# Two mixture-of-experts stages: the second layer issued behind the next expert's first layer, turns two experts ahead

## The chip, the cores and the metric

The kernel runs on one core of one Trainium2 chip. A core has a matrix engine (TensorE, "PE" in the profile, its weight loads "PEld"), a vector engine ("DVE"), a scalar engine ("ACT"), a general engine ("POOL") and a sync engine ("SP") that here only issues transfers; each engine works through its own queue in order, and the engines wait for each other through semaphores. The metric is device time in microseconds (us) for one execution of the whole kernel; lower is better.

## The reference

Eight blocks follow each other on an activation x of 4 x 1024 x 128 (4096 tokens): gated linear attention, a mixture of experts, causal attention, the same mixture again, rotary attention, a dense feed-forward block, attention with linear biases, the same dense block. What matters here is the mixture:

```python
tokens = inputs.reshape(-1, H)                       # 4096 x 128
residual = tokens
tokens = _layer_norm(tokens, ln_gamma, ln_beta)
logits = tokens @ gate_weight.T
top1 = jnp.argmax(logits, axis=-1)                   # one of E = 8 experts
...
keep = rank < CAPACITY                               # CAPACITY = 256 rows per expert
dispatch = jnp.zeros((E, CAPACITY, H)).at[top1, slot].add(tokens * keep[:, None])
h = jax.nn.gelu(jnp.einsum('ech,ehi->eci', dispatch, wi), approximate=False)   # 128 -> 512
expert_out = jnp.einsum('eci,eih->ech', h, wo)                                 # 512 -> 128
combined = weight[:, None] * expert_out[top1, slot]
out = (residual + combined).reshape(inputs.shape)
```

So each expert takes 256 rows of 128 features through a layer to 512, a Gelu, and a layer back to 128. It happens twice in the kernel, each time in a stage of its own: the next block's normalisation needs every token.

## The kernel before

x stays in SBUF for the whole kernel as 32 tiles of 128 tokens. `dispatch` (L328) runs beside the attention that precedes a mixture: it normalises, gates and ranks the tokens and scatters the rows with indirect transfers into a DRAM tensor `slots`, 256 rows per expert. `experts` (L465) is the stage that changes. It is called twice, at L1362 (after the gated linear attention) and at L1372 (after the causal attention), each time with PSUM pools of its own: four single banks of 512 columns, handed out in turn by `k.bank()` (L60), and two pairs of banks handed out by `k.banks()` (L63).

For each of the 8 experts, in this order:

1. a load of the expert's 256 rows into `given` (L472, issued by SP, 128 KB, a buffer for each expert), which waits for all scatters;
2. two transposes on TensorE (L480) into a bank: the "turn";
3. the affine part of the normalisation on DVE, out of the bank into `givenT` (L482);
4. the first layer on TensorE (L485), 4 products of 256 columns into a pair of banks; in fp32 each product shows as two matmul passes in the profile, so "x8";
5. Gelu on ACT (L493), the pair of banks into `hid`;
6. the second layer (L497), 8 products of 128 columns into a bank, "x16" in the profile;
7. a copy on DVE out of the bank into `answer` (L505), and a transfer to the DRAM tensor `answers`, issued by ACT (L506).

`givenT`, `hid` and `answer` have two buffers each. After the experts, 32 indirect gathers on POOL (L510) fetch each token's row from `answers`, and DVE adds it, weighted, to x (L516). The framework orders each engine's instructions by the order in the program and by its own estimate of when their inputs are there, puts in the semaphore waits, and lets a tile in a reused buffer or pool wait for the last use of what lay there. In the first call ACT's queue also holds four loads of `halves` (L558) for the causal attention.

Of the kernel before, what the change touches and what calls it, by code (L numbers as in the profile page):

```python
# [13 lines left out]
F32 = mybir.dt.float32  # L14
# [6 lines left out]
P = 128  # L21
# [5 lines left out]
NE, CAP, NI = 8, 256, 512  # L27
# [437 lines left out]
def experts(k: Core, m: Experts, which, weights, pool):  # L465

    nc, x = k.nc, k.x
    answers = m.answers[which]
    for e, (wi, wo) in enumerate(weights):
        rows = slice(e * CAP, (e + 1) * CAP)  # L470
        given = pool.tile([P, CAP // P, P], F32, tag="given", name="given", bufs=NE)
        load = nc.sync.dma_start(given, m.slots[rows, :].rearrange("(a p) f -> p a f", p=P))  # L472
        for name in m.sent:
            k.tc.add_manual_dep(
                load.ins, name,
                mybir.DependencyInfo(mybir.DependencyClass.Sync, mybir.DependencyReason.DATA),
            )
        ps = k.bank()
        for a in range(CAP // P):
            nc.tensor.transpose(ps[:, a * P : (a + 1) * P], given[:, a, :], k.ident)  # L480
        givenT = pool.tile([P, CAP], F32, tag="givenT", name="givenT")
        nc.vector.tensor_scalar(givenT, ps[:, :CAP], m.gamma, m.beta, ALU.mult, ALU.add)  # L482
        hps = k.banks()
        for c in range(NI // P):
            nc.tensor.matmul(  # L485
                hps[:, c * CAP : (c + 1) * CAP],
                lhsT=wi[:, c * P : (c + 1) * P],
                rhs=givenT,
                start=True,
                stop=True,  # L490
            )
        hid = pool.tile([P, NI // P, CAP], F32, tag="hid", name="hid")
        nc.scalar.activation(hid.rearrange("p c s -> p (c s)"), hps, AF.Gelu)  # L493
        ops = k.bank()
        for a in range(CAP // P):
            for c in range(NI // P):
                nc.tensor.matmul(  # L497
                    ops[:, a * P : (a + 1) * P],
                    lhsT=hid[:, c, a * P : (a + 1) * P],
                    rhs=wo[:, c, :],  # L500
                    start=(c == 0),
                    stop=(c == NI // P - 1),
                )
        answer = pool.tile([P, CAP // P, P], F32, tag="answer", name="answer")
        nc.vector.tensor_copy(answer.rearrange("p a f -> p (a f)"), ops[:, :CAP])  # L505
        nc.scalar.dma_start(answers[rows, :].rearrange("(a p) f -> p a f", p=P), answer)  # L506

    for t in range(NT):
        got = pool.tile([P, P], F32, tag="got", name="got", bufs=4)
        nc.gpsimd.indirect_dma_start(  # L510
            out=got,
            out_offset=None,
            in_=answers,
            in_offset=bass.IndirectOffsetOnAxis(ap=m.slot[:, t : t + 1], axis=0),
        )
        nc.vector.scalar_tensor_tensor(  # L516
            x[:, t, :], got, m.weight[:, t : t + 1], x[:, t, :], ALU.mult, ALU.add
        )
# [816 lines left out]
def kernel(ctx: ExitStack, tc: tile.TileContext, a: dict, out: bass.AP):  # L1335
    k = Core(ctx, tc)
    dram = ctx.enter_context(tc.tile_pool(name="dram", bufs=1, space=bass.MemoryType.DRAM))
    with tc.tile_pool(name="moe_w", bufs=1) as wp:
# [20 lines left out]
        with tc.tile_pool(name="ca_pairs", bufs=1) as rows:  # L1359
            pairs = Pairs(k, rows, dram, "ca", 6, 1)  # L1360
            with k.psum("moe0", 4, 2), tc.tile_pool(name="moe0", bufs=2) as pool:
                experts(k, m[0], 0, weights[0], pool)  # L1362
            first.close()
            causal_attention(
                k, pairs, a["ca_wq"], a["ca_wk"], a["ca_wv"], a["ca_wo"],
                lambda pool, b: dispatch(k, m[0], pool, "1", b, ("d_z", "d_zT")),
            )
        with (
            k.psum("moe1", 4, 2), tc.tile_pool(name="moe1", bufs=2) as pool,
            tc.tile_pool(name="moe1_w", bufs=1) as weights,  # L1370
        ):
            experts(k, m[0], 1, m[0].load(k, weights), pool)  # L1372
# [147 lines left out]
```

## Time and profile before

| what | us |
|---|---|
| median of 3 runs (lowest to highest) | 2838.01 (2831.23 to 2841.02) |
| the profiled execution | 2828.45 |
| its span in the trace | 2826.7 |
| first experts stage: first turn to first gather | 331.53 to 389.29 |
| its gathers, to the last addition to x | 389.29 to 431.05 |
| second experts stage: first turn to first gather | 1447.64 to 1502.14 |
| its gathers, to the last addition to x | 1502.14 to 1544.89 |
| mean granted TensorE clock over the span | 0.887 |

The profile is one execution. Rows of its timeline give start, duration, engine, line and operation, and in brackets how long the engine had been idle and what released it. "PEclk" is the granted TensorE clock as a share of full speed. Time in the two experts stages counts in full towards the total where the first gather waits for the last answer.

### The profile page before, as it was taken

What the parts mean: (1) busy time and instruction counts of PE and PEld (TensorE: products, weight loads), DVE (VectorE), ACT (ScalarE), POOL (GpSimd) and SP (SyncE); (2) the same over time, 40 slices, a digit from 0 to 9 for tenths busy, and PEclk for the clock granted to TensorE, in tenths of its full rate; (3) what the DMA queues carried; (4) which work ended last, traced back from release to release, by engine and by line L of the source; (5) the groups of instructions that cost most, each with busy time, mean ns of one, the idle gap of its engine ahead of it and who ended that gap; (6) DMA issues with size and microseconds to landing.
All of it is one profiled execution on the core that took longest, in us unless ns stands there. A gap on an engine that the chain in (4) does not pass through costs nothing.

```text
span 2826.7 us, 40396 instructions
## 1 busy us (share of the span) xinstructions
PE 2262.1 (80%) x14251; PEld 1251.0 (44%) x14251; DVE 1651.9 (58%) x4807; ACT 1260.5 (45%) x2058; POOL 1080.2 (38%) x825
## 2 busy tenths in 40 slices
PE   4676336999989989989841799935999999998898
PEld 3554223444334334333331366723544454444666
DVE  4777117676766767764211665545776777772644
ACT  5542201354545544554320265620354555555775
POOL 3754330578667767768614233241000000000222
PEclk8888575899989989999976899975799999999999
DMA  4000113110110021000112100023210212000000
GB/s 126 29 9 8 38 36 121 45 52 17 56 59 17 17 83 32 17 23 2 60 32 60 54 1 1 1 56 107 83 47 16 91 32 91 28 6 2 5 12 16
DMA packets 71000, 112.25 MB, mean 40 GB/s; under 512 B 13868, under 2 KB 45870, under 8 KB 70786
## 3 DMA queue, kind: packets, MB, share of 16 engines
q1 hardware_dynamic: 57828, 93.18, 10.4%
q0 software_dynamic: 4096, 8.40, 1.0%
q10 hardware_dynamic: 8862, 7.95, 1.0%
q8 instruction: 118, 1.93, 0.3%
q14 instruction: 96, 0.79, 0.1%
HBM read 62.29 MB, written 42.99 MB: 37 GB/s over the span
## 4 chain that ended last, share of the span: by engine, by line
PE 50%; DVE 11%; issue 11%; POOL 8%; ACT 5%; DMA 4%; SPq 1%; ACTq 0%; POOLq 0%; DVEq 0%
PE bank L590 8%; PE o L994 7%; PE o L828 6%; PE bank L1247 6%; PE scores L590 6%; DVE nm L623 3%; POOL e_first L846 3%; DVE junk L618 3%; PE scores L596 2%; PE bank L792 2%; PE bank L777 1%; PE bank L497 1%; PE banks L485 1%; PE banks L1247 1%; PE bank L858 1%
## 5 line engine op out<-in xcount | busy, mean ns | idle before, releaser
L713 ACT ACTIVATE e<-scores 128x1024 f32<-128x1024 f32 (+3 forms) x704 | 544.7, 792 | 588.0 <-PE scores L596 352.8
L846 POOL TENSOR_TENSOR e_first<-e_first,e 128x1024 f32<-128x1024 f32 (+3 forms) x320 | 538.6, 1712 | 282.2 <-PE o L828 154.1
L618 DVE CUSTOM_DVE_ANT_0 junk<-bank,mask 128x128 f32<-128x128 f32 (+3 forms) x1024 | 495.4, 484 | 228.1 <-PE bank L590 161.4
L623 DVE TENSOR_REDUCE nm<-bank 128x1 f32<-128x512 f32 x512 | 331.3, 685 | 124.6 <-PE bank L590 119.3
L828 PE MATMUL o<-e,v 128*32 128x512 f32 (+3 forms) x2560 | 297.1, 493 | 0.0
L590 PE MATMUL bank<-aa_k,aa_q 62*128 62x512 f32 (+3 forms) x768 | 237.2, 429 | 44.1 <-DVE nm L623 26.4
L994 PE MATMUL o<-e,v 128*32 128x512 f32 (+3 forms) x1536 | 223.3, 508 | 0.0
L590 PE MATMUL bank<-ca_k,ca_q 62*128 62x512 f32 (+3 forms) x768 | 191.0, 419 | 28.4 <-DVE nm L618 13.9
L590 PE MATMUL scores<-ca_q,ca_k 64*128 64x512 f32 (+3 forms) x768 | 180.3, 445 | 40.1 <-ACT e L713 38.0
L590 PEld LDWEIGHTS scores<-ca_q,ca_k 64*128 64x128 f32 x768 | 77.0, 187 | 269.9 <-ACT e L713 189.6
L596 PE MATMUL scores<-halves 64*128 64x128 f32 x2048 | 195.5, 258 | 0.0
L596 PEld LDWEIGHTS scores<-halves 64*128 64x128 f32 x2048 | 189.0, 192 | 8.8 <-issue 0.5
L965 POOL TENSOR_TENSOR lo<-val,hi 128x512 fp32r<-128x512 f32 x16 | 20.1, 1273 | 423.5 <-ACT hi L964 401.5
L590 PEld LDWEIGHTS bank<-aa_k,aa_q 62*128 62x128 f32 x768 | 120.6, 200 | 108.9 <-DVE nm L623 54.7
L590 PE MATMUL scores<-aa_q,aa_k 64*128 64x512 f32 (+3 forms) x768 | 163.3, 409 | 2.7 <-ACT e L713 2.5
L1293 DVE TENSOR_TENSOR h<-val,h 128x512 fp32r<-128x512 f32 x128 | 90.6, 715 | 121.6 <-ACT h L1292 88.0
L1237 POOL CAST h<-gate 128x512 fp32r<-128x512 f32 x32 | 26.5, 828 | 340.9 <-DVE gate L1270 335.2
L866 DVE RECIPROCAL raw<-raw 128x128 f32<-128x128 f32 x128 | 117.5, 937 | 54.4 <-ACT raw L862 45.0
L1247 PE MATMUL bank<-h,ff_h1s 128*128 128x512 f32 x512 | 134.9, 411 | 12.4 <-POOL h L1241 8.8
L590 PEld LDWEIGHTS scores<-aa_q,aa_k 64*128 64x128 f32 x768 | 79.4, 190 | 133.0 <-issue 63.0
L1287 ACT ACTIVATE val<-bank,ff_t 128x512 f32<-128x512 f32 x128 | 87.9, 689 | 97.3 <-PE bank L1247 94.1
L590 PEld LDWEIGHTS bank<-ca_k,ca_q 62*128 62x128 f32 x768 | 96.6, 202 | 75.8 <-DVE nm L618 33.2
(277 smaller groups left out, 3916.7 us busy)
## 6 DMA issues: line engine op xcount, KB each, us to landing
ca_q<-ca_q SPq DMA_DIRECT2D x64, 128.0 KB
ca_k<-ca_k SPq DMA_DIRECT2D x64, 128.0 KB
aa_q<-aa_q SPq DMA_DIRECT2D x64, 128.0 KB
aa_k<-aa_k SPq DMA_DIRECT2D x64, 128.0 KB
wi<-in_moe_wi_dram SPq DMA_DIRECT2D x16, 256.0 KB
wo<-in_moe_wo_dram SPq DMA_DIRECT2D x16, 256.0 KB
ca_q<-hi SPq DMA_DIRECT2D x8, 512.0 KB
ca_q<-lo SPq DMA_DIRECT2D x8, 512.0 KB
```

What stands on the lines that cost most here:

```text
L590: self.k.nc.tensor.matmul(out, lhsT=lhsT, rhs=rhs, start=True, stop=stop, skip_group_check=True)
L596: self.k.nc.tensor.matmul(ps, lhsT=part[:, 0, :], rhs=part[:, 1, :], start=False, stop=(a == 1), skip_group_check=True,)
L618: nc.vector.tensor_tensor_reduce(junk[:, :cols], ps[:, :cols], self.mask[:, 512 - cols :], -1.0, 3e38, ALU.add, ALU.min, to,)
L623: nc.vector.tensor_reduce(to, ps[:, :cols], AX.X, ALU.max, negate=True)
L713: nc.scalar.activation(e[:, :, :w], ps[:, :, :w], AF.Exp, scale=scale)
L828: nc.tensor.matmul(outs[which][32 * i : 32 * i + 32, skip:], lhsT=v[:, j, i, 32 * which : 32 * which + 32], rhs=es[i // 2][:, i % 2, : 512 ...
L846: nc.gpsimd.tensor_add(to, to, es[i][:, :, : 512 - skip])
L866: nc.vector.reciprocal(part, part)
L994: nc.tensor.matmul(o[32 * i : 32 * i + 32, skip:], lhsT=v[:, j, 4 * r + i, :], rhs=es[i // 2][:, i % 2, : 512 - skip], start=(j == 0), sto ...
L1247: nc.tensor.matmul(ps, lhsT=weights[:, c, :], rhs=inputs[c][i], start=(s == 0), stop=(s == len(steps) - 1))
L1287: nc.scalar.activation(val, ps, AF.Gelu, scale=s[:, o : o + 1])
L1293: nc.vector.tensor_sub(nxt[1][:, o, :], val, hi.bitcast(F32))
```

## The change

It touches `experts` alone. All eight loads of `given` are issued first. The body of the loop is cut into three functions: `turned` (transposes and `givenT`, now three buffers), `inner` (first layer and Gelu) and `outer` (second layer, copy, transfer of the answer). A new loop calls them so that the turn of expert e+2 and the first layer of expert e+1 are issued ahead of the second layer of expert e. The transfer of an answer is issued by SP instead of ACT. What is computed, and the number of instructions of each kind, stay the same.

```diff
-    for e, (wi, wo) in enumerate(weights):
-        rows = slice(e * CAP, (e + 1) * CAP)
-        given = pool.tile([P, CAP // P, P], F32, tag="given", name="given", bufs=NE)
-        load = nc.sync.dma_start(given, m.slots[rows, :].rearrange("(a p) f -> p a f", p=P))
+    given = []
+    for e in range(NE):
+        t = pool.tile([P, CAP // P, P], F32, tag="given", name="given", bufs=NE)
+        load = nc.sync.dma_start(
+            t, m.slots[e * CAP : (e + 1) * CAP, :].rearrange("(a p) f -> p a f", p=P)
+        )
...
+        given.append(t)
+
+    def turned(e):
         ps = k.bank()
         for a in range(CAP // P):
-            nc.tensor.transpose(ps[:, a * P : (a + 1) * P], given[:, a, :], k.ident)
-        givenT = pool.tile([P, CAP], F32, tag="givenT", name="givenT")
+            nc.tensor.transpose(ps[:, a * P : (a + 1) * P], given[e][:, a, :], k.ident)
+        givenT = pool.tile([P, CAP], F32, tag="givenT", name="givenT", bufs=3)
         nc.vector.tensor_scalar(givenT, ps[:, :CAP], m.gamma, m.beta, ALU.mult, ALU.add)
+        return givenT
+
+    def inner(e, givenT):
         hps = k.banks()
...
         nc.scalar.activation(hid.rearrange("p c s -> p (c s)"), hps, AF.Gelu)
+        return hid
+
+    def outer(e, hid):
         ops = k.bank()
...
         nc.vector.tensor_copy(answer.rearrange("p a f -> p (a f)"), ops[:, :CAP])
-        nc.scalar.dma_start(answers[rows, :].rearrange("(a p) f -> p a f", p=P), answer)
+        nc.sync.dma_start(
+            answers[e * CAP : (e + 1) * CAP, :].rearrange("(a p) f -> p a f", p=P), answer
+        )
+
+
+    ready = [turned(0), turned(1)]
+    hid = inner(0, ready.pop(0))
+    for e in range(NE):
+        if e + 2 < NE:
+            ready.append(turned(e + 2))
+        nxt = inner(e + 1, ready.pop(0)) if e + 1 < NE else None
+        outer(e, hid)
+        hid = nxt
```

More of the change, by code (lines that the diff above doesn't have):

```diff
@@ L485, in experts @@
             nc.tensor.matmul(
[L486 to L490, printed above, removed]
+                hps[:, c * CAP : (c + 1) * CAP], lhsT=weights[e][0][:, c * P : (c + 1) * P], rhs=givenT,
+                start=True, stop=True,
             )
@@ L497, in experts @@
                 nc.tensor.matmul(
[L498 to L502, printed above, removed]
+                    ops[:, a * P : (a + 1) * P], lhsT=hid[:, c, a * P : (a + 1) * P],
+                    rhs=weights[e][1][:, c, :], start=(c == 0), stop=(c == NI // P - 1),
                 )
```

## The prediction

> **What bounds the kernel now.** I read the page first. No engine sets the whole span; the chain that ended last runs half over TensorE (PE), and each stage has its own limit. The two layers of the experts are in that chain with 1% each, so what can be won here is some tens of us at most:
>
> ```profile
> span 2826.7 us, 40396 instructions
> ...
> PE 50%; DVE 11%; issue 11%; POOL 8%; ACT 5%; DMA 4%; SPq 1%; ACTq 0%; POOLq 0%; DVEq 0%
> ```
>
> Then the chain in order of time inside the second experts stage. Columns: start, length, engine and operation. One expert is these pieces, one behind the other, and the next expert repeats them:
>
> ```profile
> 1472.24 2.07 PE bank L497 x16
> 1474.36 0.20 issue
> 1474.61 0.06 issue
> 1474.67 0.55 DVE givenT L482
> 1475.26 2.01 PE banks L485 x8
> 1477.35 1.03 ACT hid L493
> 1478.42 2.07 PE bank L497 x16
> ```
>
> From 1472.24 to 1478.42 is 6.18: second layer, turn, givenT, first layer, Gelu, with no two of them at once. The timeline of the first stage says the same with the idle times in brackets:
>
> ```profile
> 349.85 1.99 PE L485 MATMUL banks<-givenT,wi 128*128 128x256 f32 x8 [0.75 <-DVE givenT L482]
> ...
> 353.02 2.05 PE L497 MATMUL bank<-wo,hid 128*128 128x128 f32 x16 [1.17 <-ACT hid L493]
> ...
> 354.91 0.38 PE L480 MATMUL bank<-ident,given 128*128 128x128 f32 x2
> 355.11 0.42 DVE L505 COPY answer<-bank 128x256 f32<-128x256 f32 x1 [5.31 <-PE bank L497]
> 355.45 0.54 DVE L482 TENSOR_SCALAR givenT<-bank,gamma,beta 128x256 f32<-128x256 f32 x1
> ```
>
> PE idles twice per expert, 0.75 for givenT and 1.17 for Gelu; ACT and DVE idle over 5 in each 6.19. The stage is bound by the latency of one expert's chain. That its end counts is shown by the first gather, POOL idle until the last answer has landed:
>
> ```profile
> 386.05 0.42 DVE L505 COPY answer<-bank 128x256 f32<-128x256 f32 x1 [5.31 <-PE bank L497]
> 386.50 0.37 ACTq L506 DMA_DIRECT2D answers<-answer  x1
> 389.29 1.00 POOL L510 DMA_INDIRECT got<-answers,slot  x1 [49.44 <-DMA answers<-answer]
> ```
>
> After it come 32 gathers at 1.25, DVE's additions, and only then (431.73, 1545.09) the next block's loads on SP. Nothing runs beside that, so an earlier end moves all the rest forward.
>
> **The change, part by part.** *Order.* The built kernel has on PE: turns 0, 1, 2, first layers 0 and 1, second layer 0, then turn e+3, first layer e+2, second layer e+1, and so on, ending with first layer 7, second layers 6 and 7. On all other engines, and past the stage, the order is the old one. So Gelu(e) lies beside second layer e-1, turn e+2 and first layer e+1, and givenT(e+3) beside first layer e+2.
>
> What a dense expert costs PE, from pass to pass in the rows above: first layer (1.99-0.379)/7 = 0.230 a pass (0.379 is the median pass of L485), x8 = 1.84; second layer (2.05-0.275)/15 = 0.118, x16 = 1.89; turn 0.38-0.273 = 0.107, x2 = 0.21. Sum 3.95 against 6.19. Gelu has 1.89+0.21+1.84 = 3.94 of cover for its 1.02 and about 0.15 of hand-over; DVE's 0.42+0.54 lie under 3.95 too. Without that cover they return at 1.17 and 0.75 per expert. No buffer should bite: second layer e-1 has read its `hid` before Gelu(e+1) writes there; a pair of banks is read by Gelu(e) before first layer e+2; the third `givenT` buffer is what turn e+3 needs.
>
> *First stage.* Turn 0 is at 331.53 as before. Turn 2 now stands ahead of first layer 0 and needs the third load, issued 2 x 0.47 after the first; between 0 and 1.0 of delay, I take 0.2 (givenT has to be waited for anyway until 332.89). First layer 0 runs at half clock as before (3.63), first layer 1 right behind it until 338.4. Gelu 0 waits for the table load (1.28) and is over at 339.2, as before plus 0.2. From there PE is dense: 8 second layers, 6 first layers, 5 turns and the last pass's drain: 15.14+11.04+1.07+0.16 = 27.4, end 366.6 instead of 386.0 (383.96+2.05): 19.4 saved. That is more than 7 x 2.24 = 15.7 since the old stage also ran second layer 0 at half clock (3.25) and Gelu 1 behind `halves` (0.4 late). *Second stage.* The table is loaded early. First layer 0 from 1449.1, 3.70 at half clock, first layer 1 1.84, then 27.4: end 1482.0 instead of 1499.04: 17.0 saved.
>
> *Answers on SP.* Eight issues of 0.37 per stage leave ACT's queue, where only Gelus would have stood behind them (and those would have waited for an outer layer each, had they stayed). On SP they stand behind the eight loads (over at 331.4 and 1449.3, before any answer) and ahead of loads that today start 45 us after the last answer. SP's own rows for such an issue are 0.38 to 0.47: 0 to 0.1 per stage, I take 0.
>
> *Joints.* PE rows of this stage show semaphore instructions of 0.051; three per expert, if none is hidden, 1.2 per stage; none is seen between L497 and L480 in the row above (0.115 from pass to pass), so 0 taken, 1.2 kept as an end. *Pitch.* The dense stretch of the gated linear attention at 154.93 has 20 passes of 128 in 2.40, (2.40-0.275)/19 = 0.112; by that the two stages save 1.5 more.
>
> *Clock.* Both stages start at 0.50. Changes of the granted clock lie at 336.23, 339.64 and 343.06, worked out from half-us slices, 3.41 apart; PE idling from 336.5 to 339 cost one such slice of cold clock in the first stage. Dense work leaves no such hole; a start that misses a slice would cost half of 3.41 = 1.7 per stage. The Trainium skill (TensorE: Matmul & The Clock Gate, Part 1, The HAM clock gate) has a free-running window of about 3.4 us, and the 3.41 agrees. By the same page (Part 4, PE-mode transpose) turns do not count as busy, so turns 1 and 2 ahead of the first layer would not warm the clock: by it the 1.7 could fall due, by the row (first layer alone warmed it, 332.89 to 336.23) not.
>
> **Sum.** 19.4 + 17.0 = 36.4: the profiled execution's 2828.45 becomes 2792. It lies 9.6 under the median of the runs shown, 2838.0; against the median I expect 2802 (2838.0-36.4 = 2801.6).
>
> **Rivals.** *The clock stays cold under dense work (slower).* The trace has stretches where PE looks busy and is granted little, 41.73 of 47 us at 0.54:
>
> ```profile
> 368.40:374.60 6.20, 4.26 (x26) 3.47 (x26) 0.88 (x2) 1.02 (x1) 0.00 (x0) 1.00 0.07 21
> ...
> 460.00:507.00 47.00, 41.73 (x105) 20.69 (x103) 38.39 (x131) 4.09 (x6) 0.00 (x0) 0.54 0.19 50
> ```
>
> (Columns: window, length, busy PE, PEld, DVE, ACT, POOL, clock, DMA share, GB/s.) Cold, a first layer costs 3.68, a second 3.78, a turn 0.42: the 8, 6 and 5 of them are 54.4, the ends 395 and 1511, 9 and 12 later than today: 2838+21 = 2859. It turns from gain to loss when 36.4/57.5 = 63% of the stages is cold, a mean clock under 0.68. Against it the first row: 1.00 today with PE busy 69% and two holes per expert, all the way from 343. The page named has the mechanism that would do this in a section of its own (Part 1, A second HAM failure mode: psum-queue depth-cycling): small idles between groups that cycle through banks make the clock swing; no row of the experts after 343 shows that. 4%.
>
> *Only half of the overlap.* A buffer or a wait that I read wrongly keeps first layer e+1 behind Gelu(e): then only 0.75 of 14 periods goes, 10.5 in all: 2827.5. For it: several waits hang on buffers used in turn. Against it: the counts above. 6%.
>
> *Hidden anyway.* The gathers could wait for something else than the answers, as POOL's memsets in the first stage (to 339.9) or SP: 2838. The 49.44 of idle speaks against it. 3%.
>
> **How the numbers follow.** The forecast has 87%. Its own range: down by the pitch (1.5), up by 2 x (0.8 of start + 1.2 of joints + 1.7 of clock) = 7.4, so 2800 to 2809. The rest of the kernel is entered at another phase of the clock's slices; each change of clock that falls a slice earlier or later moves it by 1.7, and the long cold stretches at 460 and 1940 to 2008 (0.50) end in such a change. The runs shown differ by 9.8 with no change at all. I add 7 above and 10 below, since the profiled execution lies that much under the median: 2790 to 2816. About 0.3%, 8.5 us, is what a measurement of this kernel can tell from no change. Faster by more: the forecast and most of the half overlap (its 10.5 is just over), 0.92; within: 0.04; slower: the cold clock, 0.04.
>
> **What would show it.** Right: from the second answer on, an expert every 3.95 on PE with no idle over 0.1 ahead of L493 and L505 (new lines of the layers), clock 1.00, Gelu over at least 2 us before its second layer; the first stage from first turn to first gather near 38.4 instead of 57.8, the second near 37.5 instead of 54.5; 32 gathers at 1.25 unchanged. Wrong: a period near 5.4 with ACT releasing PE (half overlap), a period near 7.9 with clock 0.5, or stages shorter by 36 with the same total, which would mean that a later stage gave it back.

## The result, and the profile after

| | before | after |
|---|---|---|
| median (lowest to highest) of 4 runs each | 2835.44 (2831.23 to 2841.02) | 2788.81 (2786.61 to 2798.8) |
| the profiled execution, its span | 2828.45, 2826.7 | 2786.61, 2784.8 |
| first experts stage, first turn to first gather | 57.76 | 36.93 |
| second experts stage | 54.50 | 35.12 |
| span outside both stages | 2714.4 | 2712.8 |

The ratio is 0.9844, with a 95% interval of 0.9822 to 0.9866: faster by 1.3 to 1.8%. The median lies 1.2 below the low end of the predicted range, which was set against a median before of 2838.01; as a ratio that range is 0.983 to 0.992, and the measured ratio lies in it. Of the 41.9 by which the two spans differ, the stages hold 40.2 (20.8 and 19.4), and 1.7 lies elsewhere.

The stage windows of the changed kernel's profile (window, its length, then busy PE, PEld, DVE, ACT, POOL, granted clock, DMA share, GB/s): the first stage, its gathers, the second stage.

```profile
333.36:370.29 36.93, 33.18 (x208) 30.17 (x208) 7.10 (x16) 9.36 (x9) 8.54 (x15) 0.92 0.18 48
370.29:412.10 41.81, 0.00 (x0) 0.00 (x0) 11.24 (x32) 0.00 (x0) 30.24 (x32) 0.50 0.18 50
1430.75:1465.87 35.12, 32.04 (x208) 29.44 (x208) 7.11 (x16) 8.18 (x8) 0.01 (x1) 0.94 0.18 51
```

PE runs the same 208 passes as before, now busy for 33.18 of 36.93 us where it was busy for 37.60 of 57.76, by the same window of the kernel before:

```profile
331.53:389.29 57.76, 37.60 (x208) 30.17 (x208) 7.20 (x16) 9.47 (x9) 8.32 (x14) 0.93 0.11 29
```

The gathers still take 41.81 (41.76 before): nothing was given back there. What changed inside is seen in the chain of waits in order of time, in the second stage (start, length, engine and operation):

```profile
1440.78 1.78 PE bank L505 x16
1442.56 0.22 PE bank L485 x2
1442.78 1.73 PE banks L493 x8
1444.51 1.78 PE bank L505 x16
```

Between these rows the chain no longer goes through DVE or ACT. From 1440.78 to 1444.51 one expert takes 3.73 (6.18 before), and the three pieces, second layer, turn and first layer, fill it. The timeline of the first stage shows where the other two engines went (in brackets the idle time ahead and what ended it):

```profile
346.63 0.38 PE L485 MATMUL bank<-ident,given 128*128 128x128 f32 x2
346.83 0.42 DVE L510 COPY answer<-bank 128x256 f32<-128x256 f32 x1 [2.86 <-PE bank L505]
346.85 1.89 PE L493 MATMUL banks<-givenT,wi 128*128 128x256 f32 x8
347.17 0.53 DVE L487 TENSOR_SCALAR givenT<-bank,gamma,beta 128x256 f32<-128x256 f32 x1
348.58 1.95 PE L505 MATMUL bank<-wo,hid 128*128 128x128 f32 x16
348.84 1.02 ACT L498 ACTIVATE hid<-banks 128x1024 f32<-128x1024 f32 x1 [2.71 <-PE banks L493]
350.36 0.38 PE L485 MATMUL bank<-ident,given 128*128 128x128 f32 x2
```

The PE rows carry no bracket. `givenT` (347.17 to 347.70) lies beside a first layer that does not need it, and Gelu (348.84 to 349.86) beside the second layer of the expert before; the second layer that needs it begins at 352.31, some 2.4 later. That the end of the stage still counts in full is shown by POOL's wait for the last answer:

```profile
370.29 1.00 POOL L527 DMA_INDIRECT got<-answers,slot  x1 [28.39 <-DMA answers<-answer]
```

### The profile page after: what moved, and what is told of

The parts are those of the page before. It is cut to its first block, busy times and chain, and to the rows that moved or that the text cites. A ratio compares the mean times of both kernels' runs of the same rounds, so it can differ in the third digit from the quotient of the medians.

```text
span 2784.8 us, 40381 instructions
## 1 busy us (share of the span) xinstructions
PE 2246.4 (81%) x14251; PEld 1247.6 (45%) x14251; DVE 1649.4 (59%) x4807; ACT 1259.7 (45%) x2058; POOL 1080.5 (39%) x825
## 4 chain that ended last, share of the span: by engine, by line
PE 49%; issue 12%; DVE 12%; POOL 8%; ACT 4%; DMA 3%; SPq 1%; ACTq 0%; POOLq 0%; DVEq 0%
PE bank L607 8%; PE o L1011 7%; PE o L845 6%; PE scores L607 6%; PE bank L1264 6%; POOL e_first L863 3%; DVE nm L640 3%; DVE junk L635 3%; PE scores L613 2%; PE bank L809 2%; PE bank L794 1%; PE banks L493 1%; PE bank L505 1%; POOL h L1258 1%; PE bank L875 1%
## 5 line engine op out<-in xcount | busy, mean ns | idle before, releaser
L845 PE MATMUL o<-e,v 128*32 128x512 f32 (+3 forms) x2560 | 293.1, 487 | 0.0
L607 PE MATMUL bank<-aa_k,aa_q 62*128 62x512 f32 (+3 forms) x768 | 235.1, 425 | 41.9 <-DVE nm L640 26.8
L1011 PE MATMUL o<-e,v 128*32 128x512 f32 (+3 forms) x1536 | 220.9, 504 | 0.0
```

The source lines that it names most:

```text
L607: self.k.nc.tensor.matmul(out, lhsT=lhsT, rhs=rhs, start=True, stop=stop, skip_group_check=True)
L845: nc.tensor.matmul(outs[which][32 * i : 32 * i + 32, skip:], lhsT=v[:, j, i, 32 * which : 32 * which + 32], rhs=es[i // 2][:, i % 2, : 512 ...
L1011: nc.tensor.matmul(o[32 * i : 32 * i + 32, skip:], lhsT=v[:, j, 4 * r + i, :], rhs=es[i // 2][:, i % 2, : 512 - skip], start=(j == 0), sto ...
```

## The experiments

The theory: the time went because Gelu (1.17 of PE's idle time per expert) and `givenT` (0.75) left PE's path, each by its own half of the change. The rivals: that one half did it all, that the loads issued together or the answers on SP did it, and that the gain comes from the clock at the start. In every run the two stages are read from the trace, from first turn to first gather, since the rest of the kernel is of no fixed length (below).

### The two halves alone, in program order

Turns two ahead, each expert's second layer behind its own first:

```diff
-    hid = inner(0, ready.pop(0))
     for e in range(NE):
         if e + 2 < NE:
             ready.append(turned(e + 2))
-        nxt = inner(e + 1, ready.pop(0)) if e + 1 < NE else None
-        outer(e, hid)
-        hid = nxt
+        outer(e, inner(e, ready.pop(0)))
```

> The program text has the turns two experts ahead and the second layer directly behind its own first layer, and the framework may order TensorE's queue: it puts three of the four products of the next first layer ahead of the second layer. Theory A: what counts is the built order, not the text: cover of 3 x 0.43 = 1.30 for a Gelu hole of 1.17, period 3.7 to 3.8, stages within 1 of 36.9 and 35.1, time as with the whole change. A theory by which the written order itself is needed: as strict_turns, 5.2.

The second layer late, each turn just ahead of its own first layer:

```diff
-    ready = [turned(0), turned(1)]
-    hid = inner(0, ready.pop(0))
+    hid = inner(0, turned(0))
     for e in range(NE):
-        if e + 2 < NE:
-            ready.append(turned(e + 2))
-        nxt = inner(e + 1, ready.pop(0)) if e + 1 < NE else None
+        nxt = inner(e + 1, turned(e + 1)) if e + 1 < NE else None
         outer(e, hid)
         hid = nxt
```

> The text has the second layer behind the next first layer and turns just one expert ahead; the framework splits the second layer around the next first layer, with the turn ahead of its first half. Theory A: Gelu is covered by half a second layer and a turn, 0.90 + 0.22 = 1.12 against 1.17, givenT by half a second layer, 0.90 against about 0.75, or with the answer's copy ahead of it on DVE up to 1.2: period 3.7 to 4.2, stages 37 to 41 and 35 to 39, time 0 to 8 above the whole change. If the written depth of two is what counts: as strict_late, 4.8.

Measured: turns alone 2792.82 (ratio 0.9848, 0.9828 to 0.9868), stages 39.10 and 37.48; late second layers alone 2792.43 (0.9851, 0.9831 to 0.9871), stages 39.28 and 38.38. Each half alone gives most of it: 35.7 and 34.6 of the 40.2 that the stages of the whole change give. The turns alone missed what was expected (stages within 1 of the whole change) by more than 1 in both stages: the period is 3.88 and not 3.73, and a hole is left at the end. The late second layers alone, with a period of 4.06, lie inside what was expected. The reason is the order that the framework chose. On PE, with the turns two ahead in the program, it puts three of the four products of the next first layer ahead of a second layer by itself; only the last expert, which has no next one, shows Gelu's hole (PE rows of that kernel's timeline):

```profile
353.16 2.05 PE L505 MATMUL bank<-wo,hid 128*128 128x128 f32 x16
355.05 0.38 PE L485 MATMUL bank<-ident,given 128*128 128x128 f32 x2
...
362.59 0.60 PE L493 MATMUL banks<-givenT,wi 128*128 128x256 f32 x2
364.36 2.05 PE L505 MATMUL bank<-wo,hid 128*128 128x128 f32 x16 [1.17 <-ACT hid L498]
```

With the late second layer alone it puts half of a second layer between a turn and its first layer, which hides `givenT`:

```profile
352.94 0.38 PE L485 MATMUL bank<-ident,given 128*128 128x128 f32 x2
353.38 1.16 PE L505 MATMUL bank<-wo,hid 128*128 128x128 f32 x8
354.38 1.89 PE L493 MATMUL banks<-givenT,wi 128*128 128x256 f32 x8
```

So these two runs do not separate the halves. The order had to be forced.

### The two halves alone, in a forced order

The program orders as above, and each matrix product of the two layers (in the second kernel the turns too) is bound behind the one issued before it, by a dependency that orders and adds no semaphore:

```diff
+    def put(made, behind):
+        if behind and done:
+            k.tc.add_manual_dep(
+                made.ins, done[-1],
+                mybir.DependencyInfo(mybir.DependencyClass.NoSync, mybir.DependencyReason.DATA),
+            )
+        if behind:
+            done.append(made.ins.name)
```

> Turns two experts ahead, but TensorE is held to the second layer of expert e directly behind its own first layer. Theory A (two separate holes on TensorE, each closed by what is issued into it): the hole for givenT goes, the hole for Gelu (1.17) stays. Period 1.89 first layer with its drain + 1.18 wait + 1.89 second layer + 0.22 turn = 5.2 against 6.19 before and 3.73 with the whole change; stages from first turn to first gather near 49 and 46 (57.8 and 54.5 before, 36.9 and 35.1 with the whole change); time about 18 below the kernel before. Theory B (the gain comes from the loads issued first and from the answers' transfers leaving ACT's queue, which this kernel has too): period near 3.7, stages near 37 and 35. Theory C (it is the unbroken stream that counts, any hole left brings the old speed back): period near 6.2.

> The second layer behind the next first layer, but each turn only directly ahead of its own first layer, TensorE held to that order. Theory A: the hole for Gelu goes, the hole for givenT (0.75) stays: period turn to first layer 1.13 + first layer 1.84 + second layer 1.79 = 4.76; stages near 45 and 42.5; time about 24 below the kernel before. Theory B: period near 3.7, stages near 37 and 35. Theory C: near 6.2.

Turns two ahead, second layer right behind its own first layer (PE rows of its timeline), a period of 5.17:

```profile
356.08 2.05 PE L516 MATMUL bank<-wo,hid 128*128 128x128 f32 x16 [1.17 <-ACT hid L509]
357.97 0.38 PE L496 MATMUL bank<-ident,given 128*128 128x128 f32 x2
358.19 1.89 PE L504 MATMUL banks<-givenT,wi 128*128 128x256 f32 x8
361.25 2.05 PE L516 MATMUL bank<-wo,hid 128*128 128x128 f32 x16 [1.17 <-ACT hid L509]
```

Second layer late, turn right ahead of its own first layer, a period of 4.75 (351.95 to 356.70):

```profile
351.95 1.99 PE L504 MATMUL banks<-givenT,wi 128*128 128x256 f32 x8 [0.75 <-DVE givenT L498]
...
355.57 0.38 PE L496 MATMUL bank<-ident,given 128*128 128x128 f32 x2
356.70 1.99 PE L504 MATMUL banks<-givenT,wi 128*128 128x256 f32 x8 [0.75 <-DVE givenT L498]
358.53 1.95 PE L516 MATMUL bank<-wo,hid 128*128 128x128 f32 x16
```

Each kernel keeps exactly the hole that its half does not close. The two savings per expert, 6.19 - 5.17 = 1.02 and 6.19 - 4.75 = 1.44, add up to 2.46, which is the whole change's 6.19 - 3.73. Each saving is 0.27 more than the idle time in its bracket (0.75 and 1.17): a hole also costs the 0.16 by which the last pass ahead of it is longer than its pitch (a turn's row is 0.38 long, yet work that needs no wait starts 0.22 after it), and the first pass behind it takes 0.10 longer (1.99 against 1.89). In the stages: 50.34 and 47.02 for the first kernel, 43.46 and 43.28 for the second, against 57.76 and 54.50; savings of 14.9 and 25.5, together 40.4, against 40.2 for the whole change. In time: 2812.35 (ratio 0.9923, 0.9891 to 0.9954) and 2811.81 (0.9921, 0.9898 to 0.9943). The first gained more in time than in its stages, but its interval, 13 to 31 us, holds the 14.9.

### What came along with the change

The old order with the loads first, three `givenT` buffers and the answers on SP:

```diff
+    for e in range(NE):
+        outer(e, inner(e, turned(e)))
```

> The loads of what is given first, answers issued by SP, three givenT buffers, but the old order of turn, first layer, second layer. Theory A: no gain from these: period 6.19, stages 57.8 and 54.5, at most 0.4 less in the first, where Gelu 1 no longer stands behind an answer; time as before, within 2. Theory B: most of the gain, stages near 37 and 35.

The whole change with the answers left on ACT:

```diff
-        nc.sync.dma_start(
+        nc.scalar.dma_start(
             answers[e * CAP : (e + 1) * CAP, :].rearrange("(a p) f -> p a f", p=P), answer
         )
```

> The whole change, but the answers' transfers stay on ACT. As the prediction had it: each Gelu behind them would wait for a second layer, some 0.4 to 1.8 per expert that TensorE can't cover: stages up to 10 longer. Rival: the transfer of answer e is ready 0.45 after second layer e, Gelu e+2 is wanted only after turn and first layer (0.22 + 1.89), so nothing waits: period 3.73, stages 36.9 and 35.1, time as the changed kernel within 2.

And the changed kernel once more beside them:

> The changed kernel once more, as the measure for the others of this group: 44 to 47 below the kernel before, stages 36.9 and 35.1.

The first: 2834.89, ratio 0.9992 (0.9981 to 1.0003), and a period of 6.19 as before:

```profile
357.55 2.05 PE L505 MATMUL bank<-wo,hid 128*128 128x128 f32 x16 [1.17 <-ACT hid L498]
...
363.74 2.05 PE L505 MATMUL bank<-wo,hid 128*128 128x128 f32 x16 [1.17 <-ACT hid L498]
```

Its second stage took 54.58 (54.50 before). Its first took 60.08, where 57.8 or a little less was expected: the clock stood at 0.50 from 342.8 to 353.0 (from 339.6 to 343.1 in the kernel before), so that the second expert's layers took 3.78 and 3.56 instead of 1.99 and 2.05. So without the new order the rest is worth nothing. The second: 2799.4, 0.9865 (0.9846 to 0.9884), with stages of 36.94 and 35.85, beside 2796.64, 0.9847 (0.9827 to 0.9866), with stages of 36.93 and 36.01 for the changed kernel. The stages do not differ by more than those of the changed kernel do between profiles, so the move to SP shows no worth either, and ACT's rows in the kernel with the answers on ACT say why:

```profile
352.10 1.02 ACT L498 ACTIVATE hid<-banks 128x1024 f32<-128x1024 f32 x1 [2.71 <-PE banks L493]
354.28 0.37 ACTq L511 DMA_DIRECT2D answers<-answer  x1
355.83 1.02 ACT L498 ACTIVATE hid<-banks 128x1024 f32<-128x1024 f32 x1 [2.71 <-PE banks L493]
```

A Gelu behind an answer in the queue waits for a first layer that PE runs after that answer's second layer. The issue is over at 354.65, and the Gelu's input comes at 355.83 anyway.

### The start of a stage

From first turn to first second layer (that of expert 0) the changed kernel takes 7.65 in the first stage and, in three profiles, 6.13 to 7.02 in the second: cold passes, and in the first stage a table load on ACT. Two idle things were added to take both away: products of 512 columns whose result nobody reads, ahead of the turns, and a Gelu of one column that loads the table early.

```diff
+    ps = k.bank()
+    for _ in range(19 if which == 0 else 16):
+        nc.tensor.matmul(
+            ps, lhsT=k.ident, rhs=x[:, 0:4, :].rearrange("p t d -> p (t d)"), start=True, stop=True
+        )
+    early = pool.tile([P, 1], F32, tag="early", name="early", bufs=1)
+    nc.scalar.activation(early, m.gamma, AF.Gelu)
```

> The changed kernel with 19 and 16 idle products of 512 columns on TensorE while the scatters run (their result is not read) and a Gelu on one column that brings the table in early. If the rest of the loss is the cold start: first layer 0 at 0.22 a pass instead of 0.46 and no table load on the path: first second layer about 4.5 after the first turn instead of 7.6 and 6.1, stages near 33.8 and 33.5, time 4 to 5 below the changed kernel. If the clock is cold again by the first turn, or the idle products delay it: stages as before, time the same or up to 2 longer.

Measured: 2796.05, ratio 0.986 (0.9842 to 0.9879). The second layer came 4.67 and 4.86 after the first turn, as expected, and the second stage took 33.85. But the first stage took 39.44, longer than without. Its timeline:

```profile
338.21 1.95 PE L514 MATMUL bank<-wo,hid 128*128 128x128 f32 x16
...
344.72 1.94 ACT L507 ACTIVATE hid<-banks 128x1024 f32<-128x1024 f32 x2 [7.01 <-DMA halves<-low]
345.79 3.59 PE L514 MATMUL bank<-wo,hid 128*128 128x128 f32 x16 [3.69 <-ACT hid L507]
```

Gelu 1 stands on ACT behind the four `halves` loads, which are issued at 342.21, once POOL has made their input `low` (341.79 to 342.18), about when the changed kernel issues them too (341.93). There they stand behind Gelu 1 and cost next to nothing (below); here PE waits 3.69, falls back to half clock, and runs a second layer in 3.59. Four runs took this apart: the same with the `halves` loads issued by POOL, the changed kernel as the measure beside it, the changed kernel with only those loads moved, and idle transposes in the place of the idle products (with no early Gelu).

```diff
-                nc.scalar.dma_start(
+                (nc.gpsimd if name == "ca" else nc.scalar).dma_start(
```

```diff
+    for _ in range(88 if which == 0 else 76):
+        nc.tensor.transpose(ps[:, :P], x[:, 0, :], k.ident)
```

> The kernel with the idle products and the early one-column Gelu, and with the four halves transfers of the causal pair issued on POOL's queue instead of ACT's. If the halves transfers are what held Gelu 1 (7.01 us idle ahead of it, 3.69 of PE behind it), the first stage is as short as the second, about 33.8 us from first turn to first gather (39.44 with them on ACT), the second stays at 33.9, and the two together are 4 to 5 below the changed kernel's 36.9 and 35.1 to 36.0. The rival, that the early Gelu itself or the load of its table makes the hole: the first stage stays near 39.4. The time may hide either, since the time outside the stages has differed by 11 us between executions.

> The changed kernel once more, as the measure beside the others: stages of 36.9 and 35.1 to 36.0 us, a median between 2787 and 2799.

> The changed kernel with the four halves transfers on POOL's queue alone. Its own Gelu 1 stood 3.23 us behind them by the trace, but its second layer came up to 0.48 us late only at one place, so stages of 36.9 and 35.1 to 36.0 are expected by one theory; by the rival, that these transfers hold the Gelus of the changed kernel's first stage too, the first stage is shorter by 0.5 to 1.5 us.

> The changed kernel with idle transposes of 128 columns (88 ahead of the first stage, 76 ahead of the second) in the place of the idle products of the kernel with the early Gelu, and no early Gelu. If transposes warm the clock as products do, the granted clock is 1.00 when the first layer of expert 0 starts, its 8 passes take 1.9 and not 3.6 us, and the first second layer of the second stage starts about 4.9 us after the first turn (4.86 with products, 6.13 without). If transposes don't count as work (the Trainium skill, TensorE: Matmul & The Clock Gate, Part 4, says so of PE-mode transposes), the clock stays at 0.50 past that point, the 8 passes take 3.6 us, and the second layer starts about 6.1 us after it.

Measured, with each stage split at its first second layer:

| kernel | first stage | second stage | time |
|---|---|---|---|
| kernel before | 7.50 + 50.26 | 6.09 + 48.41 | 2835.44 |
| changed kernel, first profile | 7.65 + 29.28 | 6.13 + 28.99 | 2788.81 |
| changed kernel, second | 7.66 + 29.27 | 7.02 + 28.99 | 2796.64 |
| changed kernel, third | 7.43 + 29.27 | 6.74 + 28.98 | 2795.77 |
| idle products, early Gelu | 4.67 + 34.77 | 4.86 + 28.99 | 2796.05 |
| the same, `halves` on POOL | 4.67 + 29.00 | 5.11 + 29.37 | 2790.61 |
| `halves` on POOL alone | 6.96 + 29.11 | 6.76 + 29.33 | 2795.79 (one run) |
| idle transposes | 6.94 + 29.27 | 7.01 + 28.99 | 2784.98 (one run) |

The kernel before starts its stages as the changed one does, so the gain is not in the start: it lies behind the first second layer. There 1.6 of the first stage's 21.0 is what the old kernel lost in that stage alone, a second layer and a turn at half clock (1.3) and Gelu 1 behind the `halves` loads (0.3).

With `halves` on POOL the first stage is 33.67 instead of 39.44: the loads were the cause. The two stages together take 68.15, against 72.05 to 72.94 in the three profiles of the changed kernel, the least of any run. Its time, 2790.61 (ratio 0.9853, 0.9834 to 0.9873), cannot be told from 2795.77 (0.9851, 0.9826 to 0.9877), taken beside it. With only the `halves` loads moved the first stage is 0.6 shorter than in the third profile, a size that the rival had named; but 0.5 of it lies ahead of the first second layer, where no Gelu stands behind these loads, and 0.16 behind it. So the loads hold the changed kernel's own first stage by 0.2 at most. In both kernels with these loads on POOL the second stage is longer by 0.34 and 0.38 behind its first second layer (29.33 and 29.37 against 28.99); it comes between the last copy on DVE and the first gather (3.39 and 3.42 against 3.05), and why was not looked into.

The idle transposes missed their aim, since they were over 6.7 and 6.3 us before the turns, but the clock answered all the same. Windows of half a microsecond of that kernel (PE busy, granted clock, DMA share, GB/s):

```profile
311.50:312.00 0.50, 0.50 (x5) 0.50 0.00 0
...
316.50:317.00 0.50, 0.50 (x5) 0.60 0.36 123
317.00:317.50 0.50, 0.50 (x7) 1.00 0.00 0
...
323.50:324.00 0.50, 0.20 (x2) 1.00 0.00 0
...
326.50:327.00 0.50, 0.00 (x0) 1.00 0.00 0
327.00:327.50 0.50, 0.00 (x0) 0.64 0.07 16
```

PE did nothing but transposes from 311.04 (88 show as 88 passes, where each fp32 product shows as two), and the clock rose at 316.9, 5.9 later. With idle products in the place of the transposes, behind the same small products of the gating, it was 311.88 and 317.8, the same 5.9 (4.5 to 5.5 in the three other stretches of idle products). So the transposes warmed the clock as products do; then PE stood idle from 323.7, the clock fell at 327.1, and the first layer ran cold (3.06 and 3.78 in the two stages). The first layer was cold, as the second of the two outcomes laid down has it, but for another reason than the one given there.

### The rest of the kernel

Span less both stages, in every profile of this study:

| kernel | us |
|---|---|
| before | 2714.4 |
| changed kernel, three profiles | 2712.8, 2722.0, 2724.6 |
| the eight others with the framework's order | 2718.8, 2711.7, 2714.6, 2718.7, 2711.7, 2712.8, 2721.8, 2711.1 |
| the two in a forced order | 2712.3, 2722.8 |

One and the same kernel differs by 11.8. The stages differ by 0.9 in these three profiles, so it is not there. Two windows late in the kernel, in the attention with linear biases, of its first profile and then of its third:

```profile
2100.00:2200.00 100.00, 94.64 (x737) 50.62 (x733) 76.23 (x241) 52.98 (x77) 5.02 (x4) 1.00 0.21 73
2400.00:2500.00 100.00, 95.35 (x721) 48.82 (x719) 72.44 (x236) 53.05 (x75) 0.00 (x0) 1.00 0.04 13
```

```profile
2100.00:2200.00 100.00, 94.69 (x702) 49.72 (x694) 73.07 (x226) 49.34 (x72) 5.03 (x4) 0.95 0.21 71
2400.00:2500.00 100.00, 95.67 (x691) 48.53 (x683) 70.06 (x229) 50.51 (x72) 0.00 (x0) 0.95 0.05 15
```

At equal PE busy time fewer passes fit in where the mean clock of the 100 us was 0.95 instead of 1.00. From the first start to the last, the products of L1011 take 620.9 in the first profile, 627.2 in the second, 636.6 in the third, at mean clocks of 0.98, 0.96 and 0.95. Why the clock falls in one execution and not in another was not tried.

## Why the prediction was right, and where it was off

*The bound and the mechanism* held. The latency of one expert's chain set the stages, Gelu and `givenT` went under cover, and the forced orders show each half closing its own hole, 1.44 and 1.02 per expert.

*The period was mis-sized*: 3.95 was predicted, 3.73 measured (1.78 + 0.22 + 1.73). The step that failed is "What a dense expert costs PE, from pass to pass". It took its pitches from rows that follow a wait, and the first pass of such a burst is 0.10 longer than the others. The old kernel's timeline had one cut out:

```profile
356.04 0.48 PE L485 MATMUL banks<-givenT,wi 128*128 128x256 f32 x1 [0.75 <-DVE givenT L482]
```

That is 0.48 for a pass of 0.378. Behind other work the first layer shows 1.89 instead of 1.99, the second 1.95 instead of 2.05, so the dense pitches are (1.89 - 0.379)/7 = 0.216 and (1.95 - 0.275)/15 = 0.112, not 0.230 and 0.118. The 27.4 of dense work was 26.0 (341.01 to 367.03): 1.4 per stage, 2.8 in all. The prediction had the 0.112 from a dense stretch of another block, worth 1.5, but used it for the low end of its range only; that row was the better one.

*The start of the first stage* was right: 7.67 from first turn to first second layer worked out, 7.65 measured. *The start of the second* was worked out at 7.0 (first layers of 3.70 and 1.84 behind a turn), and measured at 6.13, 7.02 and 6.74: a spread of 0.9, less than the 1.7 set aside for the phase of the clock.

*The sum.* 36.4 predicted, 40.2 in the two stages of the first profile, 39.3 and 39.8 in the others. 2.8 of the 3.8 missing is the pitch, 0.9 the second start. The stages were named as 38.4 and 37.5 and came out at 36.93 and 35.12.

*Answers on SP* was taken at 0, and is 0. The sentence in brackets, that the Gelus behind them would have waited for a second layer each had they stayed, is wrong: the run with the answers on ACT lost nothing.

*Joints* at 0 held: the chain's pieces follow each other without one.

*The clock.* It did not stay cold under dense work: 1.00 from 339.0 on in the first stage, so that rival falls. It also stayed at 1.00 in the forced order with a hole of 1.17 per expert (PE busy 23.39 of 30 us):

```profile
345.00:375.00 30.00, 23.39 (x152) 1.00 0.09 25
```

The Trainium skill's mechanism for swings between short groups (TensorE: Matmul & The Clock Gate, Part 1, A second HAM failure mode: psum-queue depth-cycling) is thus not met at these holes. The Trainium skill's sentence that transposes do not count as busy in the same way (TensorE: Matmul & The Clock Gate, Part 4, PE-mode transpose) does not agree with the idle fp32 transposes here, under which the clock went from 0.50 to 1.00 after 5.9 us in one stage and 5.7 in the other.

*Half of the overlap* and *hidden anyway* fell with the period of 3.73 and the gather that still waits for the last answer. The period of a kernel with only `givenT` hidden, which the rival put near 5.4, is 5.17 in the forced order: the rival took off the bracket of 0.75 alone, where the hole costs 1.02.

*The total.* The range's width came from the rest of the kernel, and rightly: 11.8 between profiles of one kernel. The medians of the changed kernel in three sets of runs were 2788.81, 2796.64 and 2795.77; the first is 1.2 under the range, and the other two inside it. They lie 46.6, 40.2 and 38.4 under the medians of the kernel before in the same sets (the second had been expected 44 to 47 under). The stages hold 40.2, 39.3 and 39.8 of that, so some 6 of the first set's 46.6 were luck: more than the stages gave, and within the scatter of the rest.

## What to carry to other kernels

Where a stage is a chain of two products with a step of another engine between them, put the neighbour's product into the hole, and count the gain as the holes times the number of items. The savings of the two holes added up to that of both (1.02 + 1.44 = 2.46), but the trace's idle brackets alone (0.75 + 1.17 = 1.92) fall short of it: take a hole from start to start of the work on either side, against the same work running dense. Take the cost of a dense stretch from rows that follow other work on the engine, since a row behind a wait holds its first pass's extra. Before moving anything earlier, look at what else is in the queues it crosses: the `halves` loads cost 0.2 at most until the first second layer came 3 us sooner and Gelu 1 stood behind them, and then 5.8.

## What the runs showed of the hardware

- The first matrix pass behind a wait of PE takes 0.10 longer than the next, for 256 columns (0.48 against 0.378) and, from the rows of 2.05 and 1.95, for 128.
- Fp32 transposes raised the clock as products did: it rose 5.9 and 5.7 us after the first of a run of transposes, 4.5 to 5.9 us after the first of a run of products (four stretches). It fell 3.4 and 4.6 us after the last transpose.
- The same kernel's long attention stretch took 620.9 to 636.6 from execution to execution, at mean clocks of 0.98 to 0.95: a scatter of some 10 us beside which a gain of 4, as that of the idle products with the `halves` loads moved, is seen in the trace and not in the time.
